# Attention scores of two heads at a time in the two 64-row halves of TensorE, over pairs of PSUM banks

## The chip, the cores and the metric

The program runs on one core of a Trainium2 chip. The metric is the device time of one execution in microseconds (us). A core has TensorE (PE: matmuls, with weight loads listed as PEld), VectorE (DVE), ScalarE (ACT), GpSimd (POOL) and SyncE (SP), which here only issues DMAs. Matmuls write PSUM, which has 8 banks of 512 fp32 columns on 128 partitions; DVE and ACT read it.

## The reference

Two layers on 8 batches of 512 tokens with 256 channels, 16 heads of depth 16, everything in fp32. Cut to what matters:

```python
# layer 0: causal self-attention plus cross-attention to a context of 512 rows, then a feed-forward
x = layernorm(h)
y  = softmax(causal(q(x) @ k(x).T / 4)) @ v(x)            # "S" unit of a batch
y += softmax(qc(x) @ kc(ctx).T / 4) @ vc(ctx)             # "C" unit of a batch
h  = h + y @ Wp + bias
h  = h + bitlinear(gelu(bitlinear(h)))                    # quantised activations and weights
# layer 1: cross-attention, then a feed-forward quantised over the whole tensor
x = layernorm(h)
h = h + softmax(q(x) @ k(ctx).T / 4) @ v(ctx) @ Wo + bias # "X" unit of a batch
h = h + qlinear(gelu(qlinear(layernorm(h))))              # its scales need the maximum over all batches
```

## The kernel before

The attention is cut into 24 units (8 each of S, C and X), a unit into 4 groups of four heads, 96 groups in all (`G`). One group takes these steps.

- **Projections** (`prep_job`, matmuls at L446, half a unit at a time; `vprep_job` and `outproj_job` through `proj_tokens`, L505). Every operand is split into a high and a low part of type fp32r, and three products of parts stand for one fp32 product. GpSimd makes the parts (L238 the high one, L255 the low one). The split weights are kept in DRAM and loaded again for each unit (`load_weight`).
- **Stacks** (`stack_job`, L481 and L485). DMAs copy the parts of Q and K into a stack of four heads: Q of a head pair in 96 rows, K of the even and K of the odd head each with zeros in the other head's rows. Nine DMAs a group.
- **Maxima** (`max_one`). One matmul (L555) gives the scores of 128 queries of one head into one bank; DVE takes the row maximum, with a plain reduction (L565) in C and X, and with a custom instruction that also adds the causal mask (L560) in S. S takes only the key columns up to the diagonal.
- **Rows** (`rows_job`). The negated maxima are turned by a matmul (L584) and go by DMA (L590) into rows 124 to 127 of the stack, so that the next matmul subtracts them.
- **Exponentials** (`exp_one`). One matmul (L627) gives the transposed scores of one head and one tile of 128 keys; in S a bf16 matmul (L641) adds the mask onto the diagonal tile; ACT takes the exponential (L643) into a buffer of 512 columns.
- **Values** (`av_part`, L670). Four heads at once in the four 32-column strips of the array, in plain fp32, one part for each key tile (in S: tile 0, tiles 1 and 3, tile 2).
- Outputs go to DRAM and back (`evac_job`, `post_job`), are divided by the softmax's sums on GpSimd, and are projected.

Beside the attention run the layer norms, the feed-forward of layer 0 (`ffn0_job`, matmuls L1000 and L1063), and weight preparation; the feed-forward of layer 1 (L1413 to L1489) follows when everything else is through.

The order of the instructions on each engine is fixed when the program is written. A class `Plan` holds a rough clock for each engine and rings of free buffers; jobs are generators that go on when the plan says that their inputs are there. The main stream picks among the next value part, the next maximum (they run up to `LEAD` ahead of the exponentials) and the next exponential; a job with work for PE gets a turn after the main stream had `SHARE` = 1.25 times as long. Every PSUM bank can serve every use, with these limits at one time:

```python
CAPS = {"sm": 3, "st": 3, "av": 2, "gn": 3}  # maxima, exponentials, outputs, work beside
```

Of the kernel before, what the change touches and what calls it, by code (L numbers as in the profile page):

```python
# [7 lines left out]
F32 = mybir.dt.float32  # L8
# [14 lines left out]
VST = 20  # columns of V that one head takes: 16 of V, one of ones, three of zeros  # L23
NQK = 4  # operand stacks of four heads that are alive at once
LEAD = 38  # steps that the maxima run ahead of the exponentials
NEARLY = 5  # batches of the last feed-forward's input that are loaded ahead of its start
TURNED = 3  # batches of it that the tensor engine transposes, ahead of their quantisation
FT = 2  # token tiles that one gelu takes
BUFS = {
    # SBUF buffers that jobs take turns with  # L30
    "p": 8, "xa": 1, "xl": 1, "xlt": 2, "cxt": 2, "wraw": 1, "wq": 1, "wk": 1, "wv": 2,
    "qkt": 2, "ev": 1, "oc": 2, "rb": 1, "ys": 2, "yt": 1, "xb": 2, "fy": 1, "h": 1, "hq": 1, "hqt": 1,
    "xr": 1, "xqt": 2, "mx": 3, "vt": 2,
# [11 lines left out]
# PSUM banks at most for the scores of the maxima, of the exponentials, outputs, work beside  # L45
CAPS = {"sm": 3, "st": 3, "av": 2, "gn": 3}

# Rough times in us for the plan below: an engine's fixed cost and its rate per element.
LAT = 0.25
RATE = {  # L50
    "act": (0.055, 1 / 1200), "dve": (0.07, 1 / 960), "dve2": (0.07, 1 / 1920),
# [4 lines left out]
class Plan:  # L56
    """The order of the program. Every engine runs its instructions in the order in which they are
    traced, so the trace follows a rough clock of the engines: a job, which is a generator, yields
    the time at which what it waits for is there, and goes on once the tensor engine's clock has
    come to it. Rings hold the times at which buffers come free."""  # L60

    def __init__(self):
        self.clock = dict.fromkeys(("pe", "act", "dve", "pool", "dma"), 0.0)
        self.at = {}
        self.jobs = []
        self.rings = {tag: [0.0] * n for tag, n in BUFS.items()}
        self.banks = [(0.0, i) for i in range(8)]
        self.caps = dict(CAPS)
        self.held = {use: [] for use in CAPS}
        self.turn = 0.0  # L70

# [9 lines left out]
    def pe(self, cols, *deps):  # L81
        return self.run("pe", 0.003 + cols / 2400, *deps)

    def would(self, kind, n, *deps):
        """When op would be through."""
        fixed, rate = RATE[kind]
        return max(self.clock[kind], self.now, *(d + LAT for d in deps)) + fixed + n * rate

# [28 lines left out]
    def bank_at(self, use):  # L117
        """When a PSUM bank can be had, or None."""
        if not self.banks or not self.caps[use]:
            return None  # L120
        # Banks that its readers are not through with count, too.
        held = self.held[use] = sorted(t for t in self.held[use] if t > self.now)
        n = len(held) - self.caps[use]
        return max(self.banks[0][0], held[n] if n >= 0 else 0.0)

    def bank_take(self, use):
        self.caps[use] -= 1
        return heapq.heappop(self.banks)[1]

    def bank_give(self, use, i, t):  # L130
        self.caps[use] += 1
        self.held[use].append(t)
        heapq.heappush(self.banks, (t, i))
# [4 lines left out]
    def run_jobs(self, busy):  # L138
        """Goes on with the jobs whose time has come. One with work for the tensor engine has its
        turn after the main stream had a share; busy says whether the main stream has any."""  # L140
# [24 lines left out]
DVE_HANDICAP = 0.6  # L165


def build(tc, A, out):
# [17 lines left out]
    banks = [psum.tile([P, 512], F32, name=f"bank{i}") for i in range(8)]  # L186

    def gen_bank():
        """A PSUM bank for the work beside the main stream, and its number."""
# [10 lines left out]
    def pe_next(t=None):  # L200
        """What a job yields when its next piece is for the tensor engine."""
        return (plan.now if t is None else t + LAT, 1.0)

# [1 line left out]
    with tc.tile_pool(name="start", bufs=1) as start:  # L205
# [5 lines left out]
    ident_b = const.tile([P, P], BF16, name="ident_b")  # L211
    nc.vector.tensor_copy(ident_b, ident)
# [7 lines left out]
    mask = wp.tile([P, T], BF16, name="mask")  # L220
    nc.gpsimd.memset(mask, 0.0)
    nc.gpsimd.affine_select(
        mask[:, T - P :], mask[:, T - P :], pattern=[[-1, P]], compare_op=ALU.is_ge,
        fill=NEG, base=0, channel_multiplier=1,
    )
    mask_b = const.tile([P, P], BF16, name="mask_b")
    nc.vector.tensor_copy(mask_b, mask[:, T - P :])
    qk_bias = wp.tile([P, 6, 2], F32, name="qk_bias")
    # The stack of a group's operands, [rows, (Q, K of even heads, K of odd heads), pair, 512].
    # Rows 32 r + 16 c + d: of the heads of parity c, parts (H, L, H) of Q and (H, H, L) of K, with  # L230
    # zeros in K where the other parity's rows are. Rows 124 + 2 c, 125 + 2 c: minus the row maxima
    # in two parts, and ones in K.
    qk_t = [wp.tile([P, 3, 2, T], F32R, name=f"qk{i}") for i in range(NQK)]
    v_t = [wp.tile([P, NT, H * VST + 12], F32, name=f"v{i}") for i in range(BUFS["vt"])]

    def copy_ts(dst, src):
        """A copy on GpSimd (two operations with immediate numbers are its fast form)."""
        nc.gpsimd.tensor_scalar(dst, src, 1.0, 0.0, ALU.mult, ALU.add)  # L238

    def evacuate(dst, src, n, *deps):  # L240
        """A copy from PSUM on the engine, scalar or vector, that comes to it first."""
        if plan.would("act", n, *deps) <= plan.would("dve", n, *deps) + DVE_HANDICAP:
            nc.scalar.copy(dst, src)  # L243
            return op("act", n, *deps)
        nc.vector.tensor_copy(dst, src)
        return op("dve", n, *deps)

    def turn(dst, src):
        """dst[i, k, :] = src[:, 128 k + i], by the DMA engines."""
# [3 lines left out]
    def low_part(dst, full, high):  # L253
        """dst = full - high"""
        nc.gpsimd.tensor_tensor(dst, full, high.bitcast(F32), ALU.subtract)  # L255

    def unmagic(dst, src):
        """dst = src - MAGIC"""
        nc.gpsimd.tensor_scalar(dst, src, -MAGIC, 1.0, ALU.add, ALU.mult)  # L259

# [1 line left out]
    wscr = {}  # L262

    def load_weight(name, tag):
        """[128, 2 parts, n]: split at the first use and kept in DRAM for the ones after it."""
        src = WSRC[name]
        n = src.shape[-1]
        yield from take(tag)
        w = tile(tag, [P, 2, n], F32R, f"w_{name}")
        if name in wscr:  # L270
            nc.sync.dma_start(w.bitcast(F32), wscr[name])
            return w, dma(n)
        rtag = RAW.get(name, "wraw")
        yield from take(rtag)
        raw = tile(rtag, [P, n], F32, f"raw_{name}")
        nc.sync.dma_start(raw, src)
        yield dma(n / 2) + LAT
        nc.scalar.copy(w[:, 0], raw)
        t = op("act", n)
        low_part(w[:, 1], raw, w[:, 0])  # L280
        t = op("pool2", n, t)
        give(rtag, t)
        yield t + LAT
        wscr[name] = dram.tile([P, 2, n], F32, name=f"scr_{name}")
        nc.sync.dma_start(wscr[name], w.bitcast(F32))
        dma(n)
        return w, t

    # Where the first weights pass through: in buffers whose use comes later.
    RAW = {"Sk0": "ys", "Sq1": "ys", "Sk1": "oc", "Vs": "oc", "Cq0": "rb"}  # L290
    WSRC = {}
    for key, names in (
# [5 lines left out]
        for i, nm in enumerate(names):  # L298
            WSRC[nm] = A[key][i]

# [1 line left out]
    xlt, uses = {}, {}  # L302

    def used(key, tag, t):
        """One of the readers of xlt[key] is through."""
# [5 lines left out]
    def stats(x, nm):  # L311
        """Variance, minus the mean, and (variance + eps)^-0.5, of the rows of the token tiles."""
# [10 lines left out]
        te = plan.run("dve", 0.3)  # L323
# [3 lines left out]
        te = plan.run("pool", 1.15, te)  # L327
        return mv[:, :, 1], neg, r, te

    def normalise(dst, src, nm, r, t):  # L330
        """dst = (src - mean) * r"""
        nc.gpsimd.tensor_scalar(dst, src, nm[:, t : t + 1], 1.0, ALU.add, ALU.mult)
        nc.gpsimd.tensor_scalar(dst, dst, r[:, t : t + 1], 0.0, ALU.mult, ALU.add)
        return plan.run("pool", 0.92)

    def ln_job(key, src, nm, n_uses):
        """LN of one batch of tokens, transposed, in two parts: xlt[key] = [128, 2(parts), 2(chunks), 512]."""
# [8 lines left out]
        first = key == ("S", 0)  # the other engines have nothing else to do yet  # L346
        yield from take("fy")
        xh = tile("fy", [P, NT, C], F32R, f"xh_{nm}")
        yield from take("xl")
        xl = tile("xl", [P, NT, C], F32R, f"xl_{nm}")  # L350
        for t in range(NT):
            if first:
# [4 lines left out]
                nc.scalar.copy(xh[:, t], x[:, t])  # L357
                th = op("act", C, te)
            else:
                te = normalise(x[:, t, :], x[:, t, :], neg, r, t)  # L360
        if first:
            for t in range(NT):
                nc.vector.tensor_tensor(xl[:, t], x[:, t], xh[:, t].bitcast(F32), ALU.subtract)
                tl = op("dve", C)
            te = th
        else:
            yield te + LAT
            copy_ts(xh, x)
            te = op("pool", NT * C, te)
            low_part(xl, x, xh)  # L370
            tl = op("pool2", NT * C, te)
        give("xa", tl)
        yield from take("xlt")
        xlt[key] = tile("xlt", [P, 2, 2, T], F32R, f"xlt_{nm}")
        uses[key] = [n_uses, 0.0]
# [1184 lines left out]
```

## Time and profile before

| | |
|---|---|
| median of 3 runs | 1597.23 us (1596.05 to 1600.64) |
| profiled execution, span from first to last instruction (the page gives it no other time) | 1596.5 us |
| PE busy | 1500.6 us, 94% of the span |
| DVE busy | 1300.4 us, 81% |
| ACT busy | 1087.0 us, 68% |
| POOL busy | 832.8 us, 52% |
| DMA | 244.17 MB, mean 153 GB/s |
| granted PE clock, mean | 0.981 |

The profile page gives busy time of an engine as the time in which at least one of its instructions ran; a matmul's own length contains its way through the array, so matmuls overlap in the records and the distance between two starts is the better price. The chain of waits follows the work that ended last back through what released it. The timeline merges neighbouring instructions of one line; "x8" is a count of records, and a plain fp32 matmul leaves two records.

### The profile page before, as it was taken

How to read it: one execution, taken by the hardware profiler on the slowest of the kernel's cores; microseconds unless marked ns; L12 is line 12 of the kernel's file. 1: busy time of each engine (PE TensorE's matmuls, PEld its weight loads, DVE VectorE, ACT ScalarE, POOL GpSimd, SP SyncE). 2: the span in 40 equal slices, each digit the busy share in tenths (PEclk: the TensorE clock that was granted, in tenths of full speed). 3: DMA queues.
4: the chain of work that ended last, by engine and by line, in shares of the span. 5: the costliest groups of instructions: out<-in, count | busy, mean ns of one | idle time of the engine just before them, and what ended most of it. 6: DMA issues, size and time to landing. Idle time of an engine off the chain costs nothing.

```text
span 1596.5 us, 28434 instructions
## 1 busy us (share of the span) xinstructions
PE 1500.6 (94%) x8911; PEld 905.9 (57%) x8928; DVE 1300.4 (81%) x3038; ACT 1087.0 (68%) x1934; POOL 832.8 (52%) x1059
## 2 busy tenths in 40 slices
PE   4989999999999999999999999999999989999876
PEld 3755665655665656655566465655555546555435
DVE  6878687887888888898869987888898768786687
ACT  3547667577676777677666767767776756777694
POOL 6543452653636745669447626456657434432328
PEclk8999999999999999999999999999999999999989
DMA  4664645755666646756467545755556564553422
GB/s 134 198 176 125 172 126 131 188 144 153 174 174 182 175 113 172 179 159 171 122 163 189 151 118 157 194 139 144 146 150 180 136 198 139 155 155 103 159 68 106
DMA packets 186110, 244.17 MB, mean 153 GB/s; under 512 B 82776, under 2 KB 92248, under 8 KB 185448
## 3 DMA queue, kind: packets, MB, share of 16 engines
q1 hardware_dynamic: 185960, 242.36, 56.6%
q8 instruction: 71, 1.16, 0.3%
q14 instruction: 79, 0.65, 0.1%
HBM read 101.18 MB, written 52.15 MB: 96 GB/s over the span
## 4 chain that ended last, share of the span: by engine, by line
PE 73%; DVE 11%; DMA 5%; ACT 4%; POOL 2%; issue 2%; SPq 1%; DVEq 0%; ACTq 0%; POOLq 0%
PE bank L670 18%; PE bank L555 18%; PE bank L627 17%; PE bank L446 6%; PE bank L505 5%; DVE mx L565 3%; ACT g L1414 2%; DMA qk<-qkt 2%; DVE bank L560 2%; PE bank L1063 2%; PE bank L641 2%; PE bank L381 2%; PE bank L1000 1%; DVE mhl L576 1%; ACT p L643 1%
## 5 line engine op out<-in xcount | busy, mean ns | idle before, releaser
L643 ACT ACTIVATE p<-bank 128x512 f32<-128x512 f32 x1344 | 737.5, 603 | 342.0 <-PE bank L627 221.9
L565 DVE TENSOR_REDUCE mx<-bank 128x1 f32<-128x512 f32 x1024 | 649.1, 680 | 120.7 <-PE bank L555 117.1
L555 PE MATMUL bank<-qk 124*128 124x512 f32 (+3 forms) x1536 | 552.4, 396 | 16.8 <-DMA scrz<-zr 7.3
L627 PE MATMUL bank<-qk 128*128 128x512 f32 (+3 forms) x1536 | 525.3, 387 | 11.9 <-DMA qk<-mrow 4.6
L555 PEld LDWEIGHTS bank<-qk 124*128 124x128 f32 x1536 | 283.7, 192 | 149.6 <-issue 69.6
L670 PE MATMUL bank<-p,v 128*32 128x512 f32 (+3 forms) x3072 | 365.4, 554 | 0.3
L627 PEld LDWEIGHTS bank<-qk 128*128 128x128 f32 x1536 | 282.2, 191 | 119.9 <-issue 42.2
L560 DVE CUSTOM_DVE_ANT_0 bank<-bank,mask 128x128 f32<-128x128 f32 (+3 forms) x512 | 238.4, 517 | 74.2 <-PE bank L555 71.9
L238 POOL TENSOR_SCALAR qkt<-qkt 128x512 fp32r<-128x512 f32 x92 | 57.0, 620 | 214.9 <-ACT qkt L452 145.2
L670 PEld LDWEIGHTS bank<-p,v 128*32 128x32 f32 x3072 | 66.6, 108 | 109.2 <-issue 81.3
L255 POOL TENSOR_TENSOR qkt<-qkt 128x512 fp32r<-128x512 f32 x92 | 118.3, 1286 | 7.7
L452 ACT ACTIVATE qkt<-bank,qk_bias 128x512 f32<-128x512 f32 x96 | 66.2, 689 | 37.0 <-PE bank L446 27.0
L641 PE MATMUL bank<-ident_b,mask_b 128*128 128x256 bf16 (+1 forms) x320 | 83.9, 262 | 0.0
L560 DVE DVE_READ_ACCUMULATOR2_ANT mx<- 128x1 f32 x512 | 71.9, 140 | 0.0
L727 POOL TENSOR_TENSOR oc<-oc,rb 128x512 f32<-128x512 f32 x31 | 39.7, 1282 | 60.7 <-DMA rb<-scrz 51.5
L243 ACT COPY ev<-bank 128x512 f32<-128x512 f32 x81 | 47.3, 583 | 19.8 <-PE bank L670 15.7
L1004 DVE SCALAR_TENSOR_TENSOR h<-bank,so,bc_l_b 128x512 f32<-128x512 f32 x64 | 47.2, 740 | 8.2 <-PE bank L1000 5.3
L641 PEld LDWEIGHTS <-mask_b 128*128 128x128 bf16 x320 | 30.7, 96 | 36.4 <-issue 26.2
L1482 PE MATMUL bank<-w2q,gq 128*128 128x256 bf16 x256 | 33.5, 295 | 13.2 <-POOL gq L259 6.5
L1414 ACT ACTIVATE g<-bank,b1s,sc_x 128x512 f32<-128x512 f32 x64 | 43.0, 971 | 2.5 <-POOL y L1396 2.5
L1413 PE MATMUL bank<-tyt,w1q 128*128 128x512 bf16 x127 | 37.6, 387 | 7.5 <-DVE tyt L1393 3.2
L761 POOL TENSOR_TENSOR xb<-xb,bc_l_bp 128x256 f32<-128x256 f32 x32 | 23.2, 739 | 38.9 <-DMA xb<-in_x 38.9
(264 smaller groups left out, 2059.8 us busy)
## 6 DMA issues: line engine op xcount, KB each, us to landing
qk<-qkt SPq DMA_DIRECT2D x288, 128.0 KB
qk<-qkt SPq DMA_DIRECT2D x576, 64.0 KB
scro<-ev SPq DMA_DIRECT2D x94, 256.0 KB
oc<-scro SPq DMA_DIRECT2D x47, 256.0 KB
rb<-scrz SPq DMA_DIRECT2D x47, 256.0 KB
x_d<-xb SPq DMA_DIRECT2D x15, 512.0 KB
xa_s<-in_x SPq DMA_DIRECT2D x8, 512.0 KB
xb<-in_x SPq DMA_DIRECT2D x8, 512.0 KB
```

The source lines that it names most:

```text
L255: nc.gpsimd.tensor_tensor(dst, full, high.bitcast(F32), ALU.subtract)
L446: nc.tensor.matmul(ps, wv[:, a, k, :], xs[:, e, k, :], start=(j == 0), stop=(j == len(seq) - 1))
L452: nc.scalar.activation(full, ps, AF.Identity, bias=bias)
L505: nc.tensor.matmul(ps[:, (t - t0) * C : (t - t0 + 1) * C], lhs[:, a, k, t * P : (t + 1) * P], wv[:, e, k, :], start=(j == 0), stop=(j == l ...
L555: nc.tensor.matmul(ps[:, :n], q[:, qt * P : (qt + 1) * P], k[:, :n], start=True, stop=True)
L560: nc.vector.tensor_tensor_reduce(out=ps[:, :n], in0=ps[:, :n], in1=mask[:, T - n :], scale=1.0, scalar=-3.0e38, op0=ALU.add, op1=ALU.max, ...
L565: nc.vector.tensor_reduce(dst, ps, AX.X, ALU.max)
L627: nc.tensor.matmul(ps[:, off : off + n], k[:, kt * P : (kt + 1) * P], q[:, q0:], start=off == 0, stop=kind != "S",)
L641: nc.tensor.matmul(diag, mask_b, ident_b.unsqueeze(1).broadcast_to([P, n, P]), start=False, stop=True)
L643: nc.scalar.activation(p, ps, AF.Exp, scale=0.25)
L670: nc.tensor.matmul(banks[av_t[G]][32 * j : 32 * j + 32, T - n :], v_t[un % 2][:, kt, h * VST : h * VST + 32], p, start=(i == 0), stop=last,)
L1414: nc.scalar.activation(g[:, f, b, :], ps, AF.Gelu, scale=sx[:, 2:3], bias=b1s[:, f : f + 1])
```

## The change

- The stack now holds eight heads (half a unit, `n = G // 2`): rows 0 to 47 of the array's upper half hold the three parts (interleaved) of the heads of one parity, rows 64 to 111 those of the other, with the rows for the maxima at 48, 49 and 112, 113. No zeros are needed. Two heads are multiplied at a time, one in each half of the rows, each into its own bank of a pair. `NQK` is 3 stacks of eight heads instead of 4 of four.
- A step of the maxima or exponentials takes two heads: two matmuls for each tile, then one DVE reduction over both banks or one ACT exponential over 1024 columns. In S two tiles can share a step: (0, 2), (1), (3) for the maxima and (0), (1, 3), (2) for the exponentials.
- The causal mask is added by matmuls in both places: for each step two half-identity products of 64 rows for each head (`masks`), four matmuls a step. The custom DVE instruction is gone.
- The row maxima of eight heads are turned together; an exponential waits for the maxima of both groups of its stack.
- Value parts take two key tiles at a time (in S: tile 0, then 1 to 3): two parts a group.
- Three pairs of banks serve the scores of both kinds; the fourth pair (banks 6 and 7, `zone`) serves the outputs, one bank at a time, and the work beside, one bank at a time.
- Projections, layer-norm transposes and output projections are plain fp32 matmuls without parts. All weights stay in SBUF; the columns of the Q and K weights are reordered once at the start (`weights_job`).
- Three strided DMAs for each half of the rows fill a stack, six for eight heads, in place of eighteen.

```diff
-CAPS = {"sm": 3, "st": 3, "av": 2, "gn": 3}
+CAPS = {"sm": 2, "st": 2, "av": 1, "gn": 1}
+MAXS = {"X": [(p, (qt,)) for qt in range(NT) for p in (1, 0)]}
+MAXS["S"] = [(p, qts) for qts in ((0, 2), (1,), (3,)) for p in (1, 0)]
+EXPS = {"X": [(p, (kt,)) for kt in range(NT) for p in (0, 1)]}
+EXPS["S"] = [(p, kts) for kts in ((0,), (1, 3), (2,)) for p in (0, 1)]
+AVS = {"X": [(0, 1), (2, 3)], "S": [(0,), (1, 2, 3)]}
...
+    pairs = [psum.tile([P, 2, T], F32, name=f"pair{i}") for i in range(4)]
+    banks = [pairs[i // 2][:, i % 2] for i in range(8)]
...
 def prep_job(n):
-            seq = [(a, e, k) for a, e in PARTS for k in range(nk)]
-                nc.tensor.matmul(ps, wv[:, a, k, :], xs[:, e, k, :], start=(j == 0), stop=(j == len(seq) - 1))
-                tm = plan.pe(T)
+                nc.tensor.matmul(ps, WT[wname][:, u, k], xs[:, k, :], start=(k == 0), stop=(k == nk - 1))
+                tm = plan.pe(4 * T)
...
 def stack_job(n):
+        for r, parts in enumerate((slice(0, 4, 3), slice(1, 4, 2), slice(0, 3, 2))):
+            for c in range(2):
+                nc.sync.dma_start(
+                    dst[64 * c + r : 64 * c + 48 : 3].rearrange("p g w n -> p (g w n)"),
+                    tf[64 * c : 64 * c + 64, parts, :],
+                )
...
+    def masks(ps, c, blocks, lhs, rhs):
+        n = len(range(*blocks.indices(NT)))
+        diag = ps[:, c].rearrange("p (a b) -> p a b", b=P)[:, blocks]
+        rows = slice(64 * c, 64 * c + 64)
+        for k in range(2):
+            nc.tensor.matmul(
+                diag, lhs[rows, k], rhs[rows, k].unsqueeze(1).broadcast_to([64, n, P]), start=False, stop=k == 1
+            )
...
 def max_one(s):
-        nc.tensor.matmul(ps[:, :n], q[:, qt * P : (qt + 1) * P], k[:, :n], start=True, stop=True)
+        for off, w, qt in zip(offs, size, qts):
+            for c in range(2):
+                q, k = (qk_t[n % NQK][64 * c : 64 * c + 48, pair, x] for x in range(2))
+                nc.tensor.matmul(
+                    ps[:, c, off : off + w], q[:, qt * P : (qt + 1) * P], k[:, :w],
+                    start=off == 0, stop=kind != "S",
+                )
...
+            nc.vector.tensor_reduce(
+                mx_t[n][:, :, pair, qt], ps[:, :, off : off + w], AX.X, ALU.max, negate=True
+            )
...
 def exp_one(s):
+            for c in range(2):
+                q, k = (qk_t[n % NQK][64 * c : 64 * c + 50, pair, x] for x in range(2))
+                nc.tensor.matmul(
+                    ps[:, c, off : off + w], k[:, kt * P : (kt + 1) * P], q[:, q0:],
+                    start=off == 0, stop=kind != "S",
+                )
...
-        nc.scalar.activation(p, ps, AF.Exp, scale=0.25)
+        nc.scalar.activation(pt[:, :, :off], ps[:, :, :off], AF.Exp, scale=0.25)
```

## The prediction

> **What bounds the kernel now.** First the busy times and the chain of waits on the page.
>
> ```profile
> PE 1500.6 (94%) x8911; PEld 905.9 (57%) x8928; DVE 1300.4 (81%) x3038; ACT 1087.0 (68%) x1934; POOL 832.8 (52%) x1059
> ...
> PE 73%; DVE 11%; DMA 5%; ACT 4%; POOL 2%; issue 2%; SPq 1%; DVEq 0%; ACTq 0%; POOLq 0%
> PE bank L670 18%; PE bank L555 18%; PE bank L627 17%; PE bank L446 6%; PE bank L505 5%; DVE mx L565 3%; ACT g L1414 2%; DMA qk<-qkt 2%; DVE bank L560 2%; PE bank L1063 2%; PE bank L641 2%; PE bank L381 2%; PE bank L1000 1%; DVE mhl L576 1%; ACT p L643 1%
> ```
>
> PE carries 73% of the path. The two kinds of scores (L555, L627) are 35% of it, 559 us; value products (L670) 18%, projections (L446, L505) 11%. Busy time of PE overstates it, so I price PE by distances between starts, in the timeline of two stretches.
>
> ```profile
> 1438.42 0.40 PE L555 MATMUL bank<-qk 124*128 124x512 f32 x1
> 1438.66 0.40 PE L627 MATMUL bank<-qk 128*128 128x512 f32 x1
> 1438.90 0.39 PE L555 MATMUL bank<-qk 124*128 124x512 f32 x1
> 1439.13 0.40 PE L627 MATMUL bank<-qk 128*128 128x512 f32 x1
> 1439.36 0.39 PE L555 MATMUL bank<-qk 124*128 124x512 f32 x1
> 1439.68 1.07 PE L670 MATMUL bank<-p,v 128*32 128x512 f32 x8
> 1440.68 0.50 PE L627 MATMUL bank<-qk 128*128 128x512 f32 x1
> 1441.02 0.63 PE L555 MATMUL bank<-qk 124*128 124x512 f32 x2
> ...
> 804.81 0.23 PE L641 MATMUL bank<-ident_b,mask_b 128*128 128x128 bf16 x1
> 804.85 0.48 PE L627 MATMUL bank<-qk 128*128 128x512 f32 x1
> 805.17 0.23 PE L641 MATMUL bank<-ident_b,mask_b 128*128 128x128 bf16 x1
> ```
>
> A score of 512 columns costs 0.23 us in a run of them; four value products cost 1.00. Going into value products the last score takes 0.32, and the first score after them 0.34: 0.20 us for one excursion into the column strips. A mask costs 0.13 (0.36 from mask to mask, less one score). The chain of waits near the end shows plain fp32: 0.86 us for a product of 512 columns (two records), 0.89 for four turns of 128.
>
> ```profile
> 1480.80 0.89 PE bank L798 x8
> 1481.69 0.86 PE bank L843 x2
> ```
>
> The groups, apart by shape, show the readers of the scores: busy us and mean ns of one, then the idle time ahead and who ended it. The last two lines are the nearest rows for steps of 1024 columns.
>
> ```profile
> L643 ACT ACTIVATE p<-bank 128x512 f32<-128x512 f32 x1344 | 737.5, 603 | 342.0 <-PE bank L627 221.9 <-PE bank L641 88.6 <-PE bank L555 11.4
> L565 DVE TENSOR_REDUCE mx<-bank 128x1 f32<-128x512 f32 x1024 | 649.1, 680 | 120.7 <-PE bank L555 117.1
> ...
> L1023 DVE TENSOR_REDUCE am<-h 128x1 f32<-128x1024 f32 x32 | 38.6, 1205 | 0.0
> L1020 ACT ACTIVATE jq<-h 128x1024 bf16<-128x1024 f32 x32 | 34.4, 1074 | 0.0
> ```
>
> Both ACT and DVE wait for scores, so a cheaper score is felt.
>
> **Scores.** 2,304 products of 512 columns at 0.23 are 530 us; S adds 256 each of 384, 256 and 128 columns, by their columns 0.17 + 0.12 + 0.06, 88 us: 618. The change issues the same products, two by two in different rows and different banks. No row of this trace has two products in different rows. The nearest is L670: eight records in 1.00 us where one fp32 product on the full array (L843, two records) takes 0.86, so four column strips cost 1.16 of one. Bounds: no overlap, 0; full overlap, -309. I take -309, since L670 shows independent tiles running side by side.
>
> [...]
>
> **Masks.** 320 masks at 0.13 go (-42) and 1,536 smaller ones come, in 384 steps. Upper bound: all serial, 200, so +158. Lower: one change of type a step, 50, so +8. I take two in a row per step with the two halves side by side, 768 at 0.13, 100: +58.
>
> **Excursions.** Value parts fall from 4 (S: 3) to 2 a group, 352 to 192: 160 less at 0.20, -32. New are changes between full-array work and the row halves: the order of the instructions has some 410 round trips. Price unseen: from 0 (nothing drains) to the 0.20 of the column strips, 82. I take 82, the only row of its kind.
>
> [...]
>
> **Plain fp32.** 480 products of parts (L446) at 0.23 and 744 of 256 columns (L505) at half of it go, 196 us; 160 at 0.86 and 248 at 0.43 come, 245: +49. Transposes and row turns: 128 fp32 at 0.22 (L798: four in 0.89) for 256 of parts at about half: 0.
>
> **PE in all:** -309 + 58 - 32 + 82 + 49 = -152, so the span of 1596.5 becomes 1444. The runs' median, 1597.2, lies 0.7 above that span, too little to add.
>
> **DVE.** 1,024 reductions at 0.680 are 512 of 1024 columns at 1.205 (L1023, though from SBUF): -79. In S 512 custom instructions (264 us busy by shape) become 256 reductions of 256 to 1024 columns; on the line through 0.680 and 1.205 the four cost 3.25 us together, 64 times: 208, so -57. The order puts 50 output copies on DVE instead of 13, at 0.69: +26. DVE falls from 1300 to about 1190, 82% of 1444: as loaded as now.
>
> **ACT.** 1,344 exponentials at 0.603 are 810; 640 at 1.07 (L1020) and 64 at 0.60 are 723. It had idle time: nothing on the path. **POOL** loses the parts of tokens, outputs and weights, some 100 us, off the path. **SP and DMA:** 864 stack DMAs become 288 with the same bytes, 98 weight loads go; on the path DMA had 5%. Fewer issues could free a little, but the new ones fill 16 rows each and an exponential waits for eight heads' maxima; covered by three stacks and a lead of three groups. If that cover fails, a wait of some 7 us (the longest "qk<-qkt" piece in the chain) comes back for each of the 48 half units, 340 us at the very most. Taken at 0.
>
> **Banks.** Three pairs for both kinds of scores hold as many banks as before, but in steps twice as long, and the work beside has one bank instead of three. A reader that finishes early finds fewer filled banks. Bounds: -30 (DVE's 11% of the path shrinks with its work) to +150 (below). I take +16, about one per cent of the span: **1460 us**.
>
> **Rivals.**
>
> *The halves do not overlap.* The two products of a pair run one after the other; the rest of the sum stands: 1460 + 309 = 1769. For it: no row shows row tiles. Against: L670, and separate banks.
>
> *One bank for the work beside bounds (the other side).* Until the last feed-forward of layer 0 (19 of 24 units, now about 36 to 1145 us), each use of that bank is PE, then a wait in ACT's or DVE's queue, then the copy, and the next use can't begin before. Some 350 uses: projections 160 x 0.86 + 96 x 0.69; values and output projections 107 + 48 x 0.59 + 30 x 0.68; feed-forward 48 (L1063 and L1000 in the chain) + 64 x 0.74 + 32 x 0.47; turns 40 + 80 x 0.58: about 555 us, the copies at their rows' means. Pieces of one job are apart by the main stream's share, 1.25 x 0.86, some 150 times: 165. With 0.5 us of queue a use (half of an exponential or reduction that is in the way) it is 895 of about 1000 us and hides. It decides from about 1.2 us a use: 555 + 165 + 420 + 36 before + 410 after (the 451 us from 1145 on, shortened in proportion) = 1586; at 1.4 us, 1656. Before, with three banks, no such chain could form.
>
> *Banks and row switches eat most of it.* Stalls at the upper bound of 150 instead of 16: 1594; spread over 1530 to 1600.
>
> **How the numbers follow.** Forecast 0.56, spread 1390 to 1530 by the masks (-50, +100), the switches (-82) and the pair's price (+50, if a pair costs 1.16 of one product as the four strips do). Stalls 0.17, of which 0.14 still faster and 0.03 within. One bank 0.17, of which 0.01 within. No overlap 0.10. A measurement of this kernel can tell 0.3%, about 5 us, from no change: faster 0.56 + 0.14 = 0.70, within 0.04, slower 0.16 + 0.10 = 0.26. The range of 1370 to 1640 leaves out the no-overlap case, the worst of the one bank (0.05) and 0.05 below.
>
> **What would show it.** Right: the second product of a pair starts within 0.05 us of the first, and pairs follow at 0.23 to 0.30; PE's share of the chain falls below 70%; each S step shows about 0.26 us of masks; L670 keeps 1.00 for eight records. Wrong: pairs at 0.46 or more (first rival); idle time of PE released by ACT or DVE copies out of the fourth pair, and jobs' products waiting while scores have free banks (second); DVE above 90% busy, or a longer reduction than 1.21 us for 1024 columns out of PSUM (third).

## The result, and the profile after

The changed kernel takes **1980.24 us** (median of 4 runs, 1968.32 to 1994.82) against 1598.93 for the kernel before, measured beside it: a ratio of 1.239, 95% interval 1.233 to 1.245. It is 24% slower where the forecast was 9% faster, and above every rival. The profiled execution has a span of 1993.0 us, 396.5 more than before.

The page of the changed kernel, its busy times and the PE clock in 40 slices:

```profile
PE 1633.3 (82%) x9790; PEld 710.2 (36%) x9824; DVE 1201.2 (60%) x1711; ACT 1005.6 (50%) x1151; POOL 679.0 (34%) x941
...
PEclk9889999989999988779967898878778877879558
```

DVE (1201 us) came to where the forecast put it (1190), and ACT fell. Yet no engine is near its limit: PE went from 94% to 82% of the span, DVE from 81% to 60%. And the mean clock granted to PE fell from 0.981 to 0.850. The page's chain of waits can't be read as before: it breaks off in the last feed-forward and covers 5% of the span. The timeline of PE answers to the one shown of before.

```profile
1001.45 1.13 PE L463 MATMUL pair<-cxt_X,w_Xk 128*128 128x512 f32 x2
1002.51 0.50 PE L568 MATMUL pair<-qk 48*128 48x512 f32 x2
1002.85 0.40 PE L643 MATMUL pair<-qk 50*128 50x512 f32 x2
1003.08 0.30 PE L540 MATMUL pair<-ident,mask 64*128 64x128 bf16 x4
1003.18 0.48 PE L568 MATMUL pair<-qk 48*128 48x512 f32 x2
1005.55 0.40 PE L601 MATMUL pair<-ident_r,mhl 128*16 128x128 f32 x4 [1.89 <-DVE mhl L595]
1006.61 1.06 PE L684 MATMUL pair<-p,v 128*32 128x512 f32 x8 [0.67 <-ACT mrow L291]
1007.61 0.56 PE L643 MATMUL pair<-qk 50*128 50x384 f32 x4
```

A pair of scores (x2) can cost what one score cost: 0.23 us from L643 to the next instruction (0.34 from the L568 ahead of it), and the second product of a pair starts 2 to 4 ns after the first. Four masks take 0.10. So the array's work shrank as planned. The new thing is in brackets: PE idles 1.89 us for the row maxima's parts, which DVE makes (`mhl`), then 0.67 for ACT's copy of the turned rows out of the fourth pair. Two lines that answer to those of the readers, and PE's longest waits:

```profile
L581 DVE TENSOR_REDUCE mx<-pair 128x2 f32<-128x1024 f32 x576 | 687.4, 1218 | 332.0 <-PE pair L568 252.9 <-PE pair L540 38.6 <-ACT p L657 16.3
L657 ACT ACTIVATE p<-pair 128x1024 f32<-128x1024 f32 x640 | 639.2, 1024 | 470.7 <-PE pair L643 339.8 <-PE pair L540 113.8 <-DVE mx L581 3.6
```

```profile
PE pair L643 <- DVE mx L581: 46.7, 76, 2.2
PE pair L643 <- DMA qk<-mrow: 37.6, 14, 5.1
PE pair L1419 <- ACT g L1420: 28.9, 32, 1.6
PE pair L684 <- DVE h L1013: 22.2, 15, 2.5
PE pair L684 <- ACT qkt L468: 21.6, 24, 2.6
```

The readers wait more for PE than before (253 us against 117 on DVE, 340 against 222 on ACT) while PE waits for the readers. All three take turns in waiting, as they would with too few steps in flight between them; the experiments test that. Strange are L684 (values) waiting for DVE's `h` and ACT's `qkt`, readers of another use's bank, and the last feed-forward (L1419), which in its own timeline runs two banks, waits, and runs two more:

```profile
1857.46 1.87 PE L1419 MATMUL pair<-tyt,w1q 128*128 128x512 bf16 x4 [0.87 <-ACT g L1420]
1860.19 1.87 PE L1419 MATMUL pair<-tyt,w1q 128*128 128x512 bf16 x4 [0.87 <-ACT g L1420]
```

**One account for all runs.** From the matmul records I split each span in three. *Work*: 512 columns count 0.226 us (the closest starts in the trace before), in plain fp32 0.43 (half of L843's 0.86), fewer columns in proportion, time that two products share once. *Half clock*: what the work takes longer where the granted clock was 0.5. *Gaps*: the rest, with no product in the array.

| us | span | work | half clock | gaps | time at 0.5 |
|---|---|---|---|---|---|
| before | 1597 | 1250 | 18 | 329 | 64 |
| after | 1993 | 1061 | 221 | 711 | 598 |
| difference | +396 | -189 | +203 | +382 | |

(34 matmul records are missing in the trace after and 17 in the one before, at 0.226 us each some 8 and 4 us of work that stand under gaps.)

### The profile page after: what moved, and what is told of

Read it like the earlier page. It is cut to its first block, busy times and chain, and to the rows that moved or that the text cites. A ratio compares the mean times of both kernels' runs of the same rounds, so it can differ in the third digit from the quotient of the medians.

```text
span 1993.0 us, 26889 instructions
## 1 busy us (share of the span) xinstructions
PE 1633.3 (82%) x9790; PEld 710.2 (36%) x9824; DVE 1201.2 (60%) x1711; ACT 1005.6 (50%) x1151; POOL 679.0 (34%) x941
## 5 line engine op out<-in xcount | busy, mean ns | idle before, releaser
L581 DVE TENSOR_REDUCE mx<-pair 128x2 f32<-128x1024 f32 (+3 forms) x768 | 811.1, 1085 | 413.0 <-PE pair L568 252.9
L657 ACT ACTIVATE p<-pair 128x1024 f32<-128x1024 f32 (+1 forms) x704 | 675.7, 985 | 502.5 <-PE pair L643 339.8
L684 PE MATMUL pair<-p,v 128*32 128x512 f32 (+3 forms) x3072 | 408.5, 657 | 67.9 <-DVE h L1013 22.2
L643 PE MATMUL pair<-qk 50*128 50x512 f32 (+3 forms) x1536 | 353.8, 476 | 109.7 <-DVE mx L581 46.7
L568 PE MATMUL pair<-qk 48*128 48x512 f32 (+3 forms) x1536 | 345.3, 464 | 42.7 <-ACT p L657 18.6
L643 PEld LDWEIGHTS pair<-qk 50*128 50x128 f32 x1536 | 157.4, 207 | 317.0 <-issue 124.4
L568 PEld LDWEIGHTS pair<-qk 48*128 48x128 f32 x1536 | 153.8, 202 | 219.5 <-issue 91.7
L684 PEld LDWEIGHTS pair<-p,v 128*32 128x32 f32 x3072 | 91.1, 123 | 283.9 <-issue 167.6
L468 ACT ACTIVATE qkt<-pair,qk_bias 128x512 f32<-128x512 f32 x96 | 66.0, 688 | 143.8 <-PE pair L463 114.7
L1419 PE MATMUL pair<-tyt,w1q 128*128 128x512 bf16 x127 | 59.4, 616 | 32.5 <-ACT g L1420 28.9
L1420 ACT ACTIVATE g<-pair,b1s,sc_x 128x512 f32<-128x512 f32 x64 | 49.7, 777 | 39.1 <-PE pair L1419 34.2
L540 PE MATMUL pair<-ident,mask 64*128 64x128 bf16 (+1 forms) x768 | 67.8, 255 | 0.0
```

Source lines behind the costliest of these rows:

```text
L468: nc.scalar.activation(full, ps, AF.Identity, bias=bias)
L540: nc.tensor.matmul(diag, lhs[rows, k], rhs[rows, k].unsqueeze(1).broadcast_to([64, n, P]), start=False, stop=k == 1)
L568: nc.tensor.matmul(ps[:, c, off : off + w], q[:, qt * P : (qt + 1) * P], k[:, :w], start=off == 0, stop=kind != "S",)
L581: nc.vector.tensor_reduce(mx_t[n][:, :, pair, qt], ps[:, :, off : off + w], AX.X, ALU.max, negate=True)
L643: nc.tensor.matmul(ps[:, c, off : off + w], k[:, kt * P : (kt + 1) * P], q[:, q0:], start=off == 0, stop=kind != "S",)
L657: nc.scalar.activation(pt[:, :, :off], ps[:, :, :off], AF.Exp, scale=0.25)
```

## The experiments

Three theories: **T**, a tile of two banks is one thing for the program's waits, so a write to one bank waits for the reader of the other; **B**, one bank for the work beside is a chain; **K**, the low clock is the cause. Two more came later: **R**, the readers of three pairs are too slow to turn them over, and the stacks of eight heads, of which three are too few. Every run has the kernel before beside it on the same chip, 1596 to 1600 us. All kernels below but the last were run once. Four runs of the changed kernel lie within 26 us of each other and four of the last one within 20, so a difference of less than some 25 us between single runs shows nothing by itself. An edit moves the line numbers of a kernel: L643 is L644 in most runs below.

**Two single banks for the work beside**

```diff
-    pairs = [psum.tile([P, 2, T], F32, name=f"pair{i}") for i in range(4)]
-    banks = [pairs[i // 2][:, i % 2] for i in range(8)]
+    pairs = [psum.tile([P, 2, T], F32, name=f"pair{i}") for i in range(3)]
+    banks = [pairs[i // 2][:, i % 2] for i in range(6)]
+    banks += [psum.tile([P, T], F32, name=f"bank{i}") for i in (6, 7)]
```

> The changed kernel, with banks 6 and 7 as two tiles of their own in place of one tile of two banks; nothing else moves. Theory T (a tile of two banks is one thing for the dependencies, so that work in bank 6 waits for readers of bank 7 and the other way round): the waits of value products and of the work beside on copies out of the fourth pair, about 130 us in the changed kernel's trace, fall below 50, and with the idle time some of the 598 us at half clock goes too: 1780 to 1880 us. Theory B (one bank at a time for the work beside is the chain, whatever the tiles): within 1% of 1980. Theory K (the clock alone): within 1%.

1871.36 us, 109 less. No instruction is changed, nor the bank it uses; only the waits differ. The wait of the value products for ACT's `qkt`, 21.6 us above, is now 5.4, and that for DVE's `h` went from 22.2 to 2.2:

```profile
PE bank L685 <- ACT qkt L469: 5.4, 6, 1.1
```

T holds.

**Single banks for the last feed-forward, too**

```diff
+    psum_stack.close()
+    psum2 = ctx.enter_context(tc.tile_pool(name="psum2", bufs=1, space=PSUM))
+    banks[:] = [psum2.tile([P, T], F32, name=f"tbank{i}") for i in range(8)]
```

(ahead of the last feed-forward; the pool of the pairs got a stack of its own, `psum_stack`, so that it can be closed)

> As e1_split4, and the last feed-forward gets eight tiles of one bank each instead of four of two. Theory T: the products of the last feed-forward no longer wait for a gelu after every second bank, the clock there comes back to full, and the stretch from the end of the attention to the end, 167 us in the changed kernel, falls to about 120: 45 us less than e1_split4. Theories B and K: the same as e1_split4, within 10 us.

1838.71 us, 33 less. L1419 (L1423 here) now runs on; its timeline merges 80 records where the pairs broke it after four:

```profile
1739.39 25.86 PE L1423 MATMUL tbank<-tyt,w1q 128*128 128x512 bf16 x80 [0.59 <-DVE tyt L1403]
```

I call this kernel the **base**; work 1072, half clock 145, gaps 619, 388 us at half clock.

**The kernel before, its eight banks as halves of four tiles**

```diff
-    banks = [psum.tile([P, 512], F32, name=f"bank{i}") for i in range(8)]
+    pairs = [psum.tile([P, 2, 512], F32, name=f"pair{i}") for i in range(4)]
+    banks = [pairs[i // 2][:, i % 2] for i in range(8)]
```

> The kernel before, with its eight banks given as halves of four tiles of two banks; same instructions in the same order. Theory T: every maximum and exponential now waits for the reader of the neighbouring bank, at least 8% slower, 1730 us or more. Theories B and K: within 1% of 1599.

2806.28 us, 76% over the kernel before, with not one instruction changed. Its PE waits name the readers of the neighbour bank, maxima waiting for exponentials and the other way round:

```profile
PE pair L628 <- DVE mx L566: 108.1, 129, 2.4
PE pair L556 <- ACT p L644: 97.9, 134, 3.3
```

(In the kernel before, L627 waited 1.3 us for the maxima.)

**The kernel before, one bank for outputs and one for the work beside**

```diff
-CAPS = {"sm": 3, "st": 3, "av": 2, "gn": 3}
+CAPS = {"sm": 3, "st": 3, "av": 1, "gn": 1}
```

> The kernel before, with at most one bank at a time for the work beside and one for the outputs (its caps gn and av set to 1; single-bank tiles as before). Theory B: the chain of copies through one bank bounds, 1680 us or more. Theory T: the cap itself costs little, 1590 to 1640.

1685.0 us: the two caps alone cost 87. B holds in part, too, and part of it is the row maxima: the wait of L627 for `qk<-mrow` rises from 4.6 us, first line, to 22.9, and the turned rows pass through that one bank.

```profile
PE bank L627 <- DMA qk<-mrow: 4.6, 3, 3.5
PE bank L627 <- DMA qk<-mrow: 22.9, 11, 7.6
```

**Single banks throughout, one reader for each head**

```diff
+            for c in range(2):
+                nc.vector.tensor_reduce(
+                    mx_t[n][:, c, pair, qt : qt + 1], ps[c][:, off : off + w], AX.X, ALU.max, negate=True
+                )
```

(and the same for the exponential)

> All eight PSUM banks are tiles of one bank; the two heads' scores still go to the two halves of the array, but each head's bank is reduced, or exponentiated, by an instruction of its own (512 values in place of 1024), so it is given back when its own reader is through. Three pairs of banks stay reserved for scores, one bank for outputs and one for the work beside. Theory T (what a tile of two banks holds up is the cost, for the scores as well as for the work beside): 1700 to 1790 against 1839 with three pairs and two single banks. Rival B (the reserved single bank is what is left): within 1.5% of 1839. Rival K (the low clock comes first): within 1.5% of 1839, with the half-clock time unchanged near 388 us.

1927.91 us, 89 *more* than the base: a miss for all three. Two things became dearer. Two reductions of 512 take 2 x 0.681 = 1.36 us where one of 1024 takes 1.22, two exponentials 1.20 for 1.02:

```profile
L581 DVE TENSOR_REDUCE mx<-bank 128x1 f32<-128x512 f32 x1152 | 719.6, 681 | 308.5 <-PE bank L567 241.2 <-PE bank L539 65.6
L658 ACT ACTIVATE p<-bank 128x512 f32<-128x512 f32 x1280 | 680.7, 601 | 483.7 <-PE bank L643 353.4 <-PE bank L539 93.6 <-issue 26.2
```

And the halves often stop running side by side: with a bank each, the second product can wait for its own bank after the first has started. In the base 97% of the pairs start within 60 ns, here 67%; the work rises from 1072 to 1128.

**Any bank to any use, two for outputs and two for work beside**

```diff
-CAPS = {"sm": 2, "st": 2, "av": 1, "gn": 1}
+CAPS = {"sm": 2, "st": 2, "av": 2, "gn": 2}
```

(on the last kernel; a pair may be any two free banks)

> The kernel with single-bank tiles and one reader per head, and in addition any free bank may go to any use, as in the kernel before: two pairs at most for the maxima, two for the exponentials, two banks for outputs, two for the work beside. Theory B (one bank for the work beside is a chain, as the kernel before with one bank each showed: 1598 to 1685): 60 to 120 us less than the kernel with single-bank tiles and reserved banks. Theory T alone: within 1% of it. If both hold, the time comes to 1560 to 1680, near my forecast of 1460 plus what the start, the row transfers and the low clock still cost.

1845.01 us, 83 less than with reserved banks, as B said. But with what the separate readers cost it only gets back to the base, far from the 1560 to 1680 expected if both theories held. Any bank for any use together with one reader for a pair was not tried.

**The later-free bank of a pair first**

```diff
-            for c in range(2):
+            for c in (1, 0):
```

(on the last kernel, both kinds of scores)

> The kernel in which any use may take any single bank (1845), with one edit: of each pair of products, the one whose bank comes free later is issued first, so that the other need not wait and the two run side by side; there the first to be issued was the one whose bank came free first, and the array's work came to 1086 us at full clock, 43 us more than with pairs of banks (1043). If the lost overlap of the two halves is what ate the gain from the finer banks, the array's work goes back to 1040 to 1055 us and the time to 1760 to 1805; if the waiting for banks alone sets the time, within 1% of 1845.

1862.37 us, 17 more, which is within 1% of 1845 and inside the spread of single runs: the second expectation. 88% of the pairs now start within 60 ns (72% in the kernel that it edits) and the work falls by 21, but the gaps rise by 30. So the lost overlap alone did not keep the finer banks from paying. What moved the gaps was not found.

**Values one key tile at a time, any bank**

```diff
-AVS = {"X": [(0, 1), (2, 3)], "S": [(0,), (1, 2, 3)]}
+AVS = {"X": [(0,), (1,), (2,), (3,)], "S": [(0,), (1, 3), (2,)]}
```

> The kernel with single banks that any use may take, and in addition the products with V one key tile at a time (four matmuls), as in the kernel before, in place of two or three key tiles (eight or twelve matmuls). If long runs of products with V leave the vector and scalar engines without scores (starvation by bursts), 15 to 50 us less than without this edit; if the price of turning the array from halves to columns counts more (some 250 more turns at 0.1 to 0.2 us), 25 to 50 us more.

1862.65 us against 1845, 18 more: between the two expectations and inside the spread of single runs. Shorter bursts of value products bring no gain here; whether they save waits that the added turns of the array cost again is not shown.

**Products that nothing needs**

```diff
+            nc.tensor.matmul(
+                ps[:, c, : size[0]], q[:, qts[0] * P : (qts[0] + 1) * P], k[:, : size[0]], start=True, stop=True
+            )
```

(on the base, for each head of a step of the maxima, ahead of the real ones)

> On the kernel with three pairs and two single banks (1839): the first pair of matmuls of each step of the maxima is issued twice, which adds some 144 us of array work that nothing needs and that no reader waits for longer than 0.23 us. By K (the array is at half clock because it was not busy enough, and that is what the kernel pays) the half-clock time falls from 388 us to under 200 and the time stays at or under 1840. By starvation (readers hold the banks; the clock only follows) the dummies fill part of the gaps and add the rest: 1860 to 1960, the half-clock time above 250.

1861.31 us, 22 more (inside the spread of single runs) for 135 us of added work. Time at half clock fell from 388 to 258, its price from 145 to 97, and the gaps by 63. The clock is no first cause: with a third less time at half clock the kernel is not faster. But it is what the gaps cost on top: of 135 us of useless work, the clock paid back 48.

**A reduction of a quarter**

```diff
-                mx_t[n][:, :, pair, qt], ps[:, :, off : off + w], AX.X, ALU.max, negate=True
+                mx_t[n][:, :, pair, qt], ps[:, :, off : off + P], AX.X, ALU.max, negate=True
```

> The kernel with three pairs and two single banks (1839), with the reductions of the maxima reading only the first 128 scores of each row (the row maxima are those of a part of the keys): the vector engine is through with a pair in some 0.45 us in place of 1.1, and nothing else is edited, the order neither. Starvation by readers (the products wait for the pairs that the vector engine still reads): the waits for it, 142 us in that kernel, all but go, less half-clock time follows, and the time comes to 1600 to 1720. Rival (the chains of DMAs and of the work beside set the end): 1800 to 1839.

1760.17 us, 79 less: between the two expectations, so the readers are a part of the cause and not all. The waits move on, to ACT and to the row maxima. PE's waits in the base, then here:

```profile
PE pair L644 <- DVE mx L582: 61.7, 85, 5.3
PE pair L644 <- DMA qk<-mrow: 55.4, 15, 6.3
PE pair L569 <- DVE mx L582: 31.9, 39, 3.6
...
PE pair L569 <- ACT p L658: 19.4, 41, 2.1
```

```profile
PE pair L644 <- DMA qk<-mrow: 68.6, 17, 9.2
PE pair L569 <- ACT p L658: 38.8, 94, 2.5
PE pair L644 <- ACT p L658: 27.1, 50, 1.5
PE pair L644 <- DVE mx L582: 22.9, 10, 5.5
```

**A quarter of the exponentials as well**

```diff
-        nc.scalar.activation(pt[:, :, :off], ps[:, :, :off], AF.Exp, scale=0.25)
+        nc.scalar.activation(pt, ps[:, :, :P], AF.Exp, scale=0.25)
```

(on the last kernel; it leaves out up to three quarters of the exponentials, and the value products read the rest up to four times over)

> The kernel whose reductions read 128 of the scores (1760), in which the exponentials, too, take only the first 128 scores of each row and the products with V read those over again (part of the probabilities is left out; the array streams as many columns as before). Both readers are through with a pair in some 0.45 us. Starvation by readers: the waits for the scalar engine (110 us there) go, half-clock time falls below 200 us, 1600 to 1680. Rival (chains beside: the row maxima's DMAs, the one bank, the turns of the array between modes): 1700 to 1760.

1710.9 us, 49 less again, but in the range of the rival. With DVE at 42% and ACT at 35% of the span it is still 112 over the kernel before; the largest wait of PE left is the row maxima's DMA (69.3 us).

**Small loads at the start on ScalarE's queue**

```diff
-                    nc.sync.dma_start(dst[64 * c : 64 * c + 64, k], of[64 * k : 64 * k + 64])
+                    nc.scalar.dma_start(dst[64 * c : 64 * c + 64, k], of[64 * k : 64 * k + 64])
```

(and the same for the bias)

> The kernel with three pairs and two single banks (1839), with the sixteen small loads at the start (identity and mask for the two halves, the bias of the projections) on the scalar engine's queue in place of SyncE's, so that the first load of x is no longer behind them. If the later start of the first unit (first exponentials at 79 us against 50) hangs on that load, the first product of the scores comes 8 to 12 us earlier and the time is 8 to 15 us less; if it hangs on the one bank for the work beside, no more than 4 us less.

1844.35 us. The first score starts 6.6 us earlier (34.2 us) and the first product for the exponentials 7.3 (67.1), and the time is the same within 0.3%: the better start does not reach the end.

**An order that counts on results sooner**

```diff
-LAT = 0.25
+LAT = 0.1
```

> The kernel with three pairs and two single banks (1839), with the order written out as if a result were known 0.1 us after it is there, not 0.25, so that a product is put next in line sooner after its bank's reader. The instructions are the same. If the order of the instructions leaves the readers without work (the array does other work when a pair is about to come free), 20 to 60 us less; if the pairs are simply too few, within 1%.

1816.36 us, 22 less, inside the spread of single runs: the written order is a small part at most.

**Four groups of lead**

```diff
-LEAD = 3.0
+LEAD = 4.0
```

> The kernel with three pairs and two single banks (1839), with the maxima four groups ahead of the exponentials in place of three. A stack now has eight heads, so the row maxima of two groups have to be ready before the first exponentials of the stack, and of three groups of lead one is left as slack. If that short slack is why the exponentials wait for the row maxima's DMAs (59 us in that kernel, 5 before), that wait falls below 20 us and the time by 30 to 50 us; if not, within 1%.

1844.67 us, no gain. The wait for the row maxima goes (4.5 us are left of 55.4), as expected, and another takes its place, the maxima's wait for their stacks:

```profile
PE pair L569 <- DMA qk<-qkt: 72.2, 47, 5.9
PE pair L644 <- DVE mx L582: 52.6, 89, 2.2
```

With three stacks of eight heads a longer lead takes the stack that the exponentials have not yet let go.

**Three edits of the order**

```diff
-LEAD = 3.0
+LEAD = 4.0
-AVS = {"X": [(0, 1), (2, 3)], "S": [(0,), (1, 2, 3)]}
+AVS = {"X": [(0,), (1,), (2,), (3,)], "S": [(0,), (1, 3), (2,)]}
-LAT = 0.25
+LAT = 0.0
```

> The kernel with three pairs and two single banks (1839) with three edits of the written order together: the maxima four groups ahead, the products with V one key tile at a time, and results taken as known at once. If the order can be mended: 1730 to 1790; if the three pairs bind in any order: 1800 or more.

1848.24 us: these edits of the order do not mend it.

**Four stacks, short readers**

```diff
-NQK = 3
-LEAD = 3.0
+NQK = 4
+LEAD = 4.0
```

(on the kernel with both readers quartered, whose smaller buffers leave the room)

> The kernel with both readers quartered (1711; part of the scores is not read), with four stacks of eight heads alive in place of three, and the maxima four groups ahead in place of three. There the exponentials wait 73 us for the row maxima's DMAs, and with a longer lead alone (the full readers, 1845) the maxima waited 84 us for the stacks' DMAs instead. If the number of stacks is what holds both, the two waits together fall below 25 us and the time to 1620 to 1670, the clock following; if not, within 1% of 1711.

1630.38 us, 80 less, as expected from the number of stacks. The record shows one more wait there that the account above leaves out. Ahead of the reciprocal of the softmax's sums (`zr`), which in the written order has maxima behind it, DVE sits idle until their DMA has landed: 164.7 us in 40 waits, 10.0 in 4 before. Before, then here:

```profile
DVE zr L713 <- DMA z<-scro: 10.0, 4, 6.8
DVE zr L728 <- DMA z<-scro: 164.7, 40, 11.2
```

In these 165 us PE idles 31 (2 before); in the base it is 71 us, with 16 of PE. No run moved the reciprocal, so what it costs is open.

**Four stacks, full readers**

```diff
-NQK = 3
-LEAD = 3.0
-    "p": 7, "ev": 2, "oc": 2, "xb": 2,
+NQK = 4
+LEAD = 4.0
+    "p": 5, "ev": 1, "oc": 1, "xb": 1,
```

> The kernel with three pairs and two single banks (1839), with four stacks alive and the maxima four groups ahead; to make room, five buffers of probabilities in place of seven and one in place of two for the evacuated outputs, the gathered outputs and the residual. If the stacks' number holds the waits for the row maxima and the stacks (59 and 8 us at three groups of lead, 5 and 84 at four): 1770 to 1810; if the readers with three pairs bind: within 1%; if the lost buffers cost more than the stack brings: over 1850.

1787.29 us, 51 less than the base even with fewer buffers elsewhere.

**Four stacks and the eager order**

(`LAT = 0.1` on the last kernel)

> The two edits that helped beyond the split banks together: four stacks with four groups of lead (1787) and results taken as known after 0.1 us in the written order (1839 to 1816 alone). If their gains add up, 1760 to 1775; if both take away the same waits, 1775 to 1790. Still slower than the kernel before in either case (1598), since the waits for the two readers of the score pairs, 225 us there, are touched by neither.

1779.46 us (median of 4, 1774.28 to 1794.16), ratio to the kernel before 1.114, interval 1.104 to 1.123. That is 8 us below the kernel without the eager order, less than the spread. It is the best whole version found and still 11% slower: work 1064, half clock 119, gaps 599. PE's largest waits left are for the two readers:

```profile
PE pair L644 <- DVE mx L582: 39.5, 60, 3.8
PE pair L644 <- ACT p L658: 34.7, 63, 1.5
PE pair L569 <- DVE mx L582: 34.1, 48, 2.6
PE pair L569 <- ACT p L658: 24.1, 48, 1.2
```

**Where the lost time lies.** From the changed kernel, step by step, the clock's part included: tiles of one bank where there is no pair -142; four stacks with a longer lead -51 (-80 with short readers); shorter readers, DVE -79 and ACT -49. With all of these but for the leftover of the readers the time is 1630, 34 over the kernel before with 184 us less work. I could not make that remainder go, and its cause stays open; in it are the gaps at changes of mode (109 us there, 59 before) and the half clock (79 there, 18 before), each larger by more than the 34, and DVE's waits for the softmax's sums.

## Why the prediction was wrong

| term, us | predicted | measured | |
|---|---|---|---|
| scores | -309 | -284 | 585 to 301 |
| masks | +58 | +32 | 29 to 61 |
| projections, plain fp32 | +49 | +55 | 189 to 243 |
| transposes, row turns | 0 | +19 | 19 to 38 |
| excursions and mode changes | -32 + 82 | +47 | gaps at them, 59 to 106 |
| DVE busy | 1190 | 1201 | |
| banks (stalls) | +16 | +335 | other gaps, 382 - 47 |
| clock | not priced | +203 | |

(Terms of the work by which line's product was in the array, at full clock. How much of a gap at a change of mode is due to the change is a matter of counting: with gaps under 0.2 us alone the term is +33, with up to 0.2 us of every gap +83. "Other gaps" hold every wait of PE, those for the row maxima and for other stages too.)

- **The work was right.** The pair at the price of one, the mask steps, plain fp32 and, as counted in the table, the mode changes came within 26 us each. The rival of no overlap is refuted. The 0.30 us that the signs allow a pair at most rests on no run of this case; the next score or mask came 0.23 after a pair at the closest, 0.34 in the median with the waits.
- **The step that failed is "Banks", +16 with bounds of -30 and +150.** It counted banks (three pairs "hold as many banks as before") and their steps' length, and took the rate of PE's work as what sets the end. It missed that the diff makes the banks views of four tiles: `pairs[i // 2][:, i % 2]` decides what waits for what. The other gaps grew by 335 us in its place. The two splits gave back 142 us, and the same edit alone costs the kernel before 1208. The line stood in the diff; the prediction did not ask of it who waits for whom.
- **The bounds were an average's.** Six banks as three pairs are three things to wait for. Before, a score needed one bank back after 0.68 us; now a pair needs two at once, after 1.22. With a pair made in 0.23 us, three are full in 0.7, and each other piece of DVE's or ACT's queue in front of a reader can stop PE. That DVE's busy time was to be only 82% of the span says nothing of such waits. Quartering both readers brought 128 us. The third rival (stalls of banks and switches, 1594) named this mechanism, but put 134 us on top of the forecast where 520 came.
- **"Covered by three stacks and a lead of three groups", taken at 0, was wrong by the same kind of slip.** The lead is counted in groups, the rows are needed by stacks of two: of three groups one was slack. Measured, 37.6 us of waits for the row maxima, and 51 to 80 us of time with a fourth stack and the longer lead. My upper bound of 340 had named the place.
- **The second rival holds in part.** One bank each for outputs and the work beside costs the kernel before 87 us, any bank for any use took 83 off the kernel with one reader a bank, and its own sign, "idle time of PE released by ACT or DVE copies out of the fourth pair", is in the profile after. But splitting that pair, which leaves each use its one bank, took most of that sign away, and tiles, stacks and readers took the time beyond its 1656.
- **The clock was not in the sum.** With the gaps (329 to 711 us) the time at half the clock rose (64 to 598 us), which made 203 of the 585 us lost beside the work. It is no first cause: the useless products took away a third of the half-clock time (388 to 258 us) and did not make the kernel faster. But it adds to what the gaps cost.
- The sign "PE's share of the chain falls below 70%" came true (50% in the base) and would not have told a faster kernel from this one.

## What to carry to other kernels

Before an engine's work is shortened, ask for each buffer between it and its readers how many *separate* things can be waited for, how long one is held, and which tile a view belongs to: halves of one tile waited for each other here. Halving the maker's time while making the readers' steps twice as long and the buffers half as many turned a bound into a lockstep. And what is saved on PE can be lost again in the clock: here 189 us of work were saved and half clock took 203 more, the mean granted clock going from 0.981 to 0.850 as PE's busy share fell from 94% to 82%.

## What the runs showed of the hardware

- Two products of 512 columns in rows 0 to 49 and 64 to 113 of the array start 2 to 4 ns apart (four of five pairs in the trace after). At full clock the next score or mask follows a pair after 0.23 us at the closest, the price of one on all rows in the trace before, and after 0.34 in the median, waits included.
- Between products of the whole array and of the row halves PE left 0.09 us empty going in (median); coming back, and from halves to column strips, 0.09 at the least and some 0.2 in the median, waits for other engines included.
- In the changed kernel the granted clock changes between 1 and 0.5 at edges that lie whole multiples of 3.41 us apart. It fell 75 times (10 in the kernel before). The 3.41 us before a fall had a product in the array for 35% of its time (median; 45% at the ninth decile), those before a return 88% (79% at the first). Only 11 of the 75 falls came within 4 us of a gap of over 3 us. Most came after several shorter ones: the 3.41 us before a fall had six gaps, the longest of them 1.4 us (medians).
- One reduction of 1024 columns out of two PSUM banks takes 1.22 us, two of 512 together 1.36; for the exponential 1.02 and 1.20.
